# A residual layer with a mean and a condition: another split of the bias, mean and chunk work over four engines

## The chip, the cores and the metric

The kernel runs on one core of one Trainium2 chip, and no other core takes part. The metric is device time in microseconds (us); a comparison uses the median of several executions. One further execution was recorded by the hardware profiler, and all durations of single instructions come from that one.

The engines have two names each here: TensorE is PE in the profile (its weight loads are PEld), VectorE is DVE, ScalarE is ACT, GpSimd is POOL, and SyncE is SP, which only issues transfers. SBUF is the on-chip memory; PSUM is the eight banks that TensorE writes its results to. Each engine executes its own instructions in a fixed order, and waits where an operand is not there yet.

## The reference

`x` is (4, 1024, 512), the condition `c` is (4, 256), `W` is (1536, 512) and `b` is (512), all float32. With `h = concat(c, c)` (4, 512), the reference computes

```
m[r]      = mean over l of x[r, l, :]
out[r, l] = x[r, l] + relu( x[r, l] @ W[0:512] + m[r] @ W[512:1024] + h[r] @ W[1024:1536] + b )
```

So the three last terms are one row of 512 numbers for each of the four rows r of the batch: this row is called the bias of row r below. It can only be finished when all 1024 positions of that row have been read.

## The kernel before, in words

**Tiles.** The 4096 positions are 32 tiles of 128, eight to a row of the batch. A tile's product has four chunks j of the contraction (128 each), and each float32 product is made of three faster ones: x and W are split into a high part (`hi`, `w_hi`) and a rest (`lo`, `w_lo`), and `hi*w_hi + hi*w_lo + lo*w_hi` are added up in a PSUM bank of the tile (`product`, line 459). That makes 12 matmuls of 512 columns for a tile, 3 for a chunk. There are five such banks (`O_BANKS`).

**Chunks.** The left operand has to be transposed. For the first eight tiles TensorE does that (`turn`, line 252) from x as it was loaded; for the others VectorE does it (line 254) in groups of four tiles, from a second load of x in another layout (`z`, 24 transfers of 256 KB, line 191), and writes a PSUM bank (`xT`, two banks). ScalarE takes the high part from there and sums it over the positions as it goes (`split_hi`, 265); VectorE takes the rest (`split_lo`, 281).

**Bias.** For each row, `weigh` (348, ScalarE) and `add_term` (353, GpSimd) make the two condition terms in SBUF (`cond`); `total` (336) and `mean_term` (341), both VectorE, add the four mean terms and leave the result in a PSUM bank (`acc`). `acc_split_hi` (357, ScalarE) and `acc_split_lo` (361, VectorE) split it, and `bias_product` (373, TensorE) spreads it over 128 partitions.

**Bias to tile.** For rows 0 and 1, TensorE adds the bias to the tile's bank with one more matmul (`bias_to_bank`, 470; 13 tiles), and ScalarE's relu empties the bank (480). The first three tiles (`KEEP = 3`) are finished before a bias is there: ScalarE copies them to SBUF (`keep`, 473), and VectorE adds the bias later, both operands in SBUF. For rows 2 and 3 VectorE adds the bias as it empties the bank (`add_bias`, 477) and ScalarE applies the relu. GpSimd adds x (`add_x`, 485), and SyncE stores.

**Order.** The order on each engine is not written by hand. `Plan` (line 19) is a list scheduler that runs when the kernel is built: each step has costs for the engines that may run it, the steps that it depends on, and a number that says how urgent it is; `run` takes the step that can start first by its own clock. The costs and numbers are the kernel's own constants. What comes out is one fixed sequence for each engine, also for SyncE's transfers. A row's bias product is put in TensorE's sequence where the plan's clock has it ready.

**Start.** x tiles 0, 1, 2-3 and 4-7 are loaded from SyncE's queue, the four chunks of W[0:512] from ScalarE's queue (line 202) beside them, the condition `c_sb` and `b_sb` from GpSimd's (146, 149). Eleven matmuls on zeros keep TensorE busy until x is there (144).

Of the kernel before, what the change touches and what calls it, by code (L numbers as in the profile page):

```python
# [12 lines left out]
ALU = mybir.AluOpType  # L13
AX = mybir.AxisListType
PSUM = bass.MemoryType.PSUM
N_WARM = 11


class Plan:
# [3 lines left out]


    HANDOVER = 0.2
    PATIENCE = 0.1
# [5 lines left out]
    def add(self, key, costs, deps, urgency, emit, later=0.0):  # L32


        assert key not in self.todo, key
        self.todo[key] = (costs, list(deps), urgency, emit, later)

    def run(self):
        while self.todo:
            could = []  # L40
            for key, (costs, deps, urgency, _, _) in self.todo.items():
                if not all(d in self.done for d in deps):
                    continue
                options = []
                for engine, cost in costs.items():
                    start = self.free[engine]
                    for d in deps:
                        end, later, by = self.done[d]
                        if by != engine:
                            end += later + self.HANDOVER  # L50
                        start = max(start, end)
                    options.append((start + cost, start, engine, cost))
                _, start, engine, cost = min(options)
                could.append((start, urgency, key, engine, cost))
# [14 lines left out]
def kernel(  # L69
# [8 lines left out]

# [11 lines left out]
    S_BUFS = 15  # L103
    O_BANKS = 5
    Z_BUFS = 3
    X_BUFS = 4
    O_BUFS = 10
    Z_AHEAD, X_AHEAD, T_AHEAD = 24, 8, 7
    TURN_PE = (0, 1, 2, 3)
    BY_PE = 2  # L110
    KEEP = 3
# [4 lines left out]
    spool = ctx.enter_context(tc.tile_pool(name="spool", bufs=S_BUFS))  # L116
    small = ctx.enter_context(tc.tile_pool(name="small", bufs=2))
# [16 lines left out]
    warm = const.tile([P, 512], BF16, name="warm")  # L134
    nc.vector.memset(warm, 0.0)
    ones = const.tile([P, 1], F32, name="ones")
    nc.vector.memset(ones, 1.0)
    table_warm = const.tile([P, 1], F32, name="table_warm")
    nc.scalar.activation(table_warm, ones, AF.Relu)
    ident = const.tile([P, P], F32, name="ident")  # L140
    make_identity(nc, ident)
    pw = ps_b.tile([P, 512], F32, tag="b", name="pw")
    for _ in range(N_WARM):
        nc.tensor.matmul(pw, lhsT=warm[:, :P], rhs=warm, start=True, stop=True)
    c_sb = const.tile([B, H], F32, name="c_sb")
    nc.gpsimd.dma_start(out=c_sb, in_=cond)
    b_sb = const.tile([P, D], F32, name="b_sb")
    nc.gpsimd.memset(b_sb, 0.0)
    nc.gpsimd.dma_start(out=b_sb[0:1, :], in_=b.rearrange("(o d) -> o d", o=1))
    mean32 = const.tile([P, P], F32, name="mean32")  # L150
    nc.gpsimd.memset(mean32, 1.0 / L)
    mean = const.tile([P, P], F32R, name="mean")
    nc.gpsimd.tensor_copy(mean, mean32)


    units = [(0, 0, 1), (0, 1, 1), (0, 2, 2), (0, 4, 4)]
    units += [(r, k, G) for r in range(1, B) for k in range(0, NK, G)]
    unit_of = {(r, k0 + i): u for u, (r, k0, n) in enumerate(units) for i in range(n)}
    last_tile = [r * NK + k0 + n - 1 for r, k0, n in units]
    units_of_row = [[u for u, v in enumerate(units) if v[0] == r] for r in range(B)]  # L160
    by_z = [u for u in range(len(units)) if u not in TURN_PE]

# [4 lines left out]
    first_piece = [min(c for (u, _), c in piece_of.items() if units[u][0] == r) for r in range(B)]  # L167
# [3 lines left out]
    w_x = const.tile([P, J, D], F32, name="w_x")  # L171
    w_mean = const.tile([P, J, D], F32, name="w_mean")

# [22 lines left out]
    SP = 0.72  # L196
    SPZ = 1.3
    for i, n in ((0, 1), (1, 1), (2, 2)):
        load_x(0, i, n)
        plan.done["x", 0, i] = (2.8 + 1.3 * i, 2.0, "sp")  # L200
    for j in range(J):
        nc.scalar.dma_start(out=w_x[:, j, :], in_=Wv[0, :, j])
        plan.done["w", j] = (2.9 + 1.3 * j, 2.0, "sp")
    load_x(1)
    plan.done["x", 1] = (9.8, 2.0, "sp")
    w_cond = xpool.tile([P, 2, KH, D], F32, tag="x", name="w_cond")
    nc.sync.dma_start(
        out=w_cond, in_=W[2 * D : 3 * D].rearrange("(s h p) o -> p s h o", p=P, h=KH)
    )
    plan.done["cond"] = (12.7, 2.0, "sp")  # L210
    nc.sync.dma_start(out=w_mean, in_=Wv[1])
    plan.done["w_mean"] = (15.3, 2.0, "sp")
    plan.free["sp"] = 15.3
    for n, u in enumerate(by_z):
        for i in range(NQ):
            deps = [("turn", c) for c in range(len(pieces)) if n >= Z_BUFS and pieces[c][0] == by_z[n - Z_BUFS]]
            plan.add(("z", u, i), {"sp": SPZ}, deps, units[u][0] * NK + units[u][1] - Z_AHEAD,
                     lambda e, u=u, i=i: load_z(u, i), later=3.0)
    x_order = [0, 1, None] + list(range(2, B * NK // G))
    for n, g in list(enumerate(x_order))[3:]:  # L220
        was = x_order[n - X_BUFS] if n >= X_BUFS else -1
        deps = ([] if was == -1 else [("add_cond", k) for k in range(KH)] if was is None else
                [("finished", was * G + i) for i in range(G)])
        ahead = T_AHEAD + 10 if any(u in TURN_PE for u in (unit_of[divmod(g * G, NK)],)) else X_AHEAD
        plan.add(("x", g), {"sp": 4 * SP}, deps, g * G - ahead,
                 lambda e, g=g: load_x(g), later=3.0)
# [3 lines left out]
    w_lo = const.tile([P, J, D], F32R, name="w_lo")  # L230
    for j in range(J):
        plan.add(("w_hi", j), {"act": 0.62}, [("w", j)], -100 + 2 * j,
                 lambda e, j=j: nc.scalar.activation(w_hi[:, j, :], w_x[:, j, :], AF.Copy))
        plan.add(("w_lo", j), {"dve": 0.69, "pool": 1.33}, [("w_hi", j)], -100 + 2 * j + 1,
# [9 lines left out]
    def turn(c):  # L244
        u, js = pieces[c]
        n = units[u][2]
        v = xT[c] = ps_x.tile([P, G * P], F32, tag="x", name=f"xT{c}")
        if u in TURN_PE:
            for i in range(n):
                x_t = x_tile(last_tile[u] - n + 1 + i).rearrange("p (a j) -> p j a", j=J)  # L250
                for m, j in enumerate(js):
                    nc.tensor.transpose(v[:, (m * n + i) * P : (m * n + i + 1) * P], x_t[:, j], ident)  # L252
        else:
            nc.vector.transpose(  # L254
# [15 lines left out]
    def add_up(c):  # L270
        u, js = pieces[c]
        r, n = units[u][0], units[u][2]
# [5 lines left out]
    def split_lo(c):  # L278
        u, js = pieces[c]
        m = units[u][2] * len(js) * P  # L280
        nc.vector.tensor_tensor(  # L281
            lo[c][:, :m], xT[c][:, :m], hi[c][:, :m].bitcast(F32), ALU.subtract
        )

    for c, (u, js) in enumerate(pieces):
        r, k0, n = units[u]

        urgent = 2 * c - 99.5 if not r else r * NK - T_AHEAD + (c - first_piece[r]) * 0.75
        deps = ([x_here(t) for t in range(last_tile[u] - n + 1, last_tile[u] + 1)]
                if u in TURN_PE else [("z", u, i) for i in range(NQ)])  # L290
        if c:
            deps.append(("turn", c - 1))
        if c >= 2:
            deps.append(("lo", c - 2))
            if len(pieces[c - 2][1]) > 1:
                deps.append(("sum", c - 2))
        if r == 1 and c == first_piece[1]:
            deps.append(("term", 0, KH + J - 1))
        w = n * len(js)
        plan.add(("turn", c), {"pe": 0.12 * w} if u in TURN_PE else {"dve": 0.14 + 0.24 * w}, deps, urgent,  # L300
                 lambda e, c=c: turn(c))
        deps = [("turn", c)]
        if c >= S_BUFS:
            v, js_v = pieces[c - S_BUFS]
            deps.append(("product", last_tile[v], js_v[-1]))
        plan.add(("hi", c), {"act": 0.16 + 0.2 * (len(js) == 1) + 0.108 * w}, deps, urgent,
                 lambda e, c=c: split_hi(c))
        plan.add(("lo", c), {"dve": 0.15 + 0.135 * w}, [("hi", c)], urgent - 0.1,
                 lambda e, c=c: split_lo(c))
        if len(js) > 1:  # L310
            plan.add(("sum", c), {"dve": 0.65}, [("turn", c)], urgent + 0.1, lambda e, c=c: add_up(c))
# [4 lines left out]
    bL = const.tile([P, D], F32, name="bL")  # L316
    acc, acc_hi, acc_lo, totals, terms, biases = {}, {}, {}, {}, {}, {}
    conds = {}

    def turn_cond():  # L320
        nc.vector.tensor_scalar(bL, b_sb, float(L), None, ALU.mult)
# [9 lines left out]
    def add_cond(eng, k):  # L331
        eng.tensor_tensor(wc[:, k], w_cond[:, 0, k], w_cond[:, 1, k], ALU.add)

    def total(r):
        totals[r] = small.tile([P, J], F32, tag="tot", name=f"tot{r}")
        nc.vector.tensor_reduce(totals[r], sums[:, r], AX.X, ALU.add)

    def mean_term(r, j):
        if not j:
            acc[r] = ps_b.tile([P, D], F32, tag="b", name=f"acc{r}")  # L340
        nc.vector.scalar_tensor_tensor(  # L341
            acc[r], w_mean[:, j, :], totals[r][:, j : j + 1], acc[r] if j else conds[r],
            ALU.mult, ALU.add,
        )

    def weigh(r, k):
        terms[r, k] = small.tile([P, D], F32, tag="term", bufs=3, name=f"term{r}_{k}")
        nc.scalar.activation(terms[r, k], wc[:, k], AF.Copy, scale=cT[:, k, r : r + 1])  # L348

    def add_term(r, k):  # L350
        if not k:
            conds[r] = small.tile([P, D], F32, tag="cond", bufs=B, name=f"cond{r}")
        nc.gpsimd.tensor_tensor(conds[r], conds[r] if k else bL, terms[r, k], ALU.add)  # L353

    def acc_split_hi(r):
        acc_hi[r] = small.tile([P, D], F32R, tag="acc_hi", bufs=1, name=f"acc_hi{r}")
        nc.scalar.activation(acc_hi[r], acc[r], AF.Copy)  # L357

    def acc_split_lo(r):
        acc_lo[r] = small.tile([P, D], F32R, tag="acc_lo", bufs=1, name=f"acc_lo{r}")  # L360
        nc.vector.tensor_tensor(acc_lo[r], acc[r], acc_hi[r].bitcast(F32), ALU.subtract)

    pbs, rows = {}, {}
    even32 = const.tile([2 * Q, P], F32, name="even32")
# [219 lines left out]
```

## Time and profile before

| | |
|---|---|
| three executions | 117.69, 117.67, 118.13 us; median 117.69 |
| span of the profiled execution | 115.7 us |
| time around the span (median less span; the page gives no other total for the profiled execution) | 2.0 us |
| mean granted TensorE clock | 0.985 |
| busy: PE, DVE, ACT, POOL | 107.7, 81.0, 53.4, 57.8 us |
| instructions: PE, DVE, ACT, POOL | 466, 114, 122, 55 |
| moved by DMA | 26.31 MB, mean 227 GB/s |

The span runs from the first to the last instruction of the execution. A share of busy time is an average over stages; the chain of waits, which follows the last instruction back to what released it, tells which engine sets the end. In that chain, and in the list of instructions in order of time, each line gives the start, the length, the engine, the tile and the line of code; in the list a bracket behind it gives the idle time before and what ended it.

### The profile page before, as it was taken

To read this page: it belongs to the slowest core of one execution; us is meant where nothing else is said; L and a number is where in the kernel's file an instruction comes from. 1 tells how busy PE (TensorE), PEld (TensorE's weight loads), DVE (VectorE), ACT (ScalarE), POOL (GpSimd) and SP (SyncE) were. 2 spreads that over 40 slices of the span, in tenths; PEclk is the share of its full clock that TensorE was granted. 3 is DMA by queue.
4 is the path that set the end of the run, shared out by engine and by line. 5 is a ranking of instruction groups with operands and counts; after the bars stand their busy time and mean duration, and the time that the engine had idled before them with its cause. 6 is when DMAs were issued, how large, how long until landed. Compare 5 with 4: busy or idle time off the path is not lost.

```text
span 115.7 us, 1477 instructions
## 1 busy us (share of the span) xinstructions
PE 107.7 (93%) x466; PEld 82.9 (72%) x466; DVE 81.0 (70%) x114; ACT 53.4 (46%) x122; POOL 57.8 (50%) x55
## 2 busy tenths in 40 slices
PE   5926999999999999999999999999999999999980
PEld 2415788888766687877766688887888878888870
DVE  1066734399999999976896999939999980632250
ACT  5055547887568460424963542246466140642200
POOL 6507144899809643040893029508354913199400
PEclk9998599999999999999999999999999999999999
DMA  3799999999999959999959999994422422025351
GB/s 109 179 392 396 394 370 198 203 203 205 205 256 281 199 136 207 304 388 390 349 177 213 272 397 407 400 258 176 164 91 106 169 91 91 0 91 222 140 227 45
DMA packets 22999, 26.31 MB, mean 227 GB/s; under 512 B 1228, under 2 KB 13776, under 8 KB 22864
## 3 DMA queue, kind: packets, MB, share of 16 engines
q1 hardware_dynamic: 22352, 25.17, 75.7%
q10 hardware_dynamic: 576, 1.05, 3.1%
q8 instruction: 3, 0.05, 0.2%
q14 instruction: 4, 0.03, 0.1%
q0 software_dynamic: 64, 0.01, 0.0%
HBM read 17.83 MB, written 8.39 MB: 227 GB/s over the span
## 4 chain that ended last, share of the span: by engine, by line
PE 89%; DMA 7%; SPq 1%; DVE 0%; issue 0%
PE po_None L459 77%; DMA x<-in_x_dram 7%; PE po_None L470 4%; PE xT L252 3%; PE po L459 2%; PE pb L373 2%; SPq L178 1%; PE po L455 0%; DVE o L490 0%; PE pt L324 0%
## 5 line engine op out<-in xcount | busy, mean ns | idle before, releaser
L485 POOL TENSOR_TENSOR o<-o,x 128x512 f32<-128x512 f32 x30 | 38.7, 1315 | 38.9 <-ACT o L480 32.1
L459 PE MATMUL po_None<-w_hi,hi 128*128 128x512 f32 x124 | 50.8, 409 | 0.0
L459 PE MATMUL po_None<-w_lo,hi 128*128 128x512 f32 x124 | 49.4, 398 | 0.0
L459 PE MATMUL po_None<-w_hi,lo 128*128 128x512 f32 x124 | 49.3, 398 | 0.0
L459 PEld LDWEIGHTS po_None<-w_hi,hi 128*128 128x128 f32 x124 | 23.5, 190 | 7.1 <-issue 1.6
L459 PEld LDWEIGHTS po_None<-w_hi,lo 128*128 128x128 f32 x124 | 23.6, 190 | 5.7
L459 PEld LDWEIGHTS po_None<-w_lo,hi 128*128 128x128 f32 x124 | 23.6, 190 | 5.0
L281 DVE TENSOR_TENSOR lo<-xT,hi 128x512 fp32r<-128x512 f32 (+1 forms) x34 | 21.9, 647 | 7.2 <-ACT hi L265 7.2
L254 DVE STREAM_TRANSPOSE xT<-z 128x512 f32<-128x512 f32 x24 | 26.2, 1102 | 0.3
L265 ACT ACTIVATE hi<-xT 128x512 fp32r<-128x512 f32 (+1 forms) x34 | 19.3, 571 | 9.3 <-DVE xT L254 5.5
L477 DVE TENSOR_TENSOR o<-po_None,bias 128x512 f32<-128x512 f32 x15 | 9.8, 677 | 12.2 <-ACT bias L379 4.1
L480 ACT ACTIVATE o<-o 128x512 f32<-128x512 f32 x17 | 10.5, 631 | 7.5 <-DVE o L477 7.5
L480 ACT ACTIVATE o<-po_None 128x512 f32<-128x512 f32 x13 | 7.5, 601 | 7.9 <-PE po_None L470 7.9
L341 DVE SCALAR_TENSOR_TENSOR acc<-w_mean,tot,acc 128x512 f32<-128x512 f32 x12 | 9.1, 756 | 0.4
L252 PE MATMUL xT<-ident,x 128*128 128x128 f32 x32 | 6.0, 307 | 3.5 <-DMA x<-in_x_dram 3.5
L252 PEld LDWEIGHTS xT<-ident,x 128*128 128x128 f32 x32 | 5.1, 207 | 4.6 <-issue 2.5
L357 ACT ACTIVATE acc_hi<-acc 128x512 fp32r<-128x512 f32 x4 | 2.4, 600 | 11.9 <-DVE acc L341 11.9
L265 ACT ACTIVATION_READ_ACCUMULATOR hi<-xT 128x1 f32 x32 | 6.4, 201 | 0.0
L353 POOL TENSOR_TENSOR cond<-bL,term 128x512 f32<-128x512 f32 x4 | 5.2, 1303 | 2.0 <-ACT term L348 2.0
L341 DVE SCALAR_TENSOR_TENSOR acc<-w_mean,tot,cond 128x512 f32<-128x512 f32 x4 | 5.7, 1426 | 0.6 <-POOL cond L353 0.3
L348 ACT ACTIVATE term<-wc,cT 128x512 f32<-128x512 f32 x8 | 5.6, 723 | 0.7 <-POOL cond L353 0.7
L353 POOL TENSOR_TENSOR cond<-cond,term 128x512 f32<-128x512 f32 x4 | 5.5, 1383 | 0.3
(54 smaller groups left out, 60.7 us busy)
## 6 DMA issues: line engine op xcount, KB each, us to landing
out_dram<-o SPq DMA_DIRECT2D x31, 256.0 KB, 2.4
x<-in_x_dram SPq DMA_DIRECT2D x7, 1024.0 KB, 7.9
z<-in_x_dram SPq DMA_DIRECT2D x24, 256.0 KB, 7.4
w_x<-in_L_cond_W_dram ACTq DMA_DIRECT2D x4, 256.0 KB, 7.2
w_cond<-in_L_cond_W_dram SPq DMA_DIRECT2D x1, 1024.0 KB, 12.7
w_mean<-in_L_cond_W_dram SPq DMA_DIRECT2D x1, 1024.0 KB, 12.6
x<-in_x_dram SPq DMA_DIRECT2D x2, 256.0 KB, 4.1
x<-in_x_dram SPq DMA_DIRECT2D x1, 512.0 KB, 8.0
```

The lines of the kernel that those rows point to most:

```text
L252: nc.tensor.transpose(v[:, (m * n + i) * P : (m * n + i + 1) * P], x_t[:, j], ident)
L254: nc.vector.transpose(v[:, : n * P].rearrange("p (n t) -> p n t", t=Q), zs[u].rearrange("p n (a j) -> p n j a", j=J)[:, : n * NQ, js[0], :],)
L265: nc.scalar.activation(hi[c][:, :m], xT[c][:, :m], AF.Copy, accum_out=sums[:, r, js[0], s : s + 1] if len(js) == 1 else None,)
L281: nc.vector.tensor_tensor(lo[c][:, :m], xT[c][:, :m], hi[c][:, :m].bitcast(F32), ALU.subtract)
L341: nc.vector.scalar_tensor_tensor(acc[r], w_mean[:, j, :], totals[r][:, j : j + 1], acc[r] if j else conds[r], ALU.mult, ALU.add,)
L348: nc.scalar.activation(terms[r, k], wc[:, k], AF.Copy, scale=cT[:, k, r : r + 1])
L353: nc.gpsimd.tensor_tensor(conds[r], conds[r] if k else bL, terms[r, k], ALU.add)
L459: nc.tensor.matmul(pos[key][:, :w], lhsT=v[p][:, c], rhs=m[:, j, d], start=(h is None and j == 0 and n == 0), stop=((t < KEEP or r >= BY_P ...
L470: nc.tensor.matmul(pos[t], lhsT=even, rhs=rows[t // NK], start=False, stop=True)
L477: nc.vector.tensor_tensor(o, o if t < KEEP else pos[t], biases[t // NK], ALU.add)
L480: nc.scalar.activation(o_tile(t), pos[t] if KEEP <= t < BY_PE * NK else outs[t], AF.Relu)
L485: nc.gpsimd.tensor_tensor(outs[t], outs[t], x_tile(t), ALU.add)
```

## The change

- **Loads.** The chunks of W[0:512] go over SyncE's queue, mixed with the x tiles: x 0, w 0, w 1, x 1, w 2, w 3, x 2-3, x 4-7, then the mean part and the condition part of W. `c_sb` and `b_sb` go over ScalarE's queue. Five warming matmuls stand in place of eleven. ScalarE scales `b_sb` by 1024 in place (`b_row`).
- **Bias to tile.** `bias_to_bank` is gone. Ten tiles are kept in SBUF (`KEEP = 10`); VectorE adds the bias there later. All other tiles but the last get it from VectorE as it empties the bank.
- **Mean terms.** `mean_term` on VectorE is gone: `weigh` (ScalarE) and `add_term` (GpSimd) make six terms for each row in place of two. The sum stays in SBUF, so both splits read it there.
- **Chunks.** The chunks j = 1 and j = 3 of the tiles that VectorE turns go to SBUF (`tpool`, three buffers) and not to PSUM; three of these twelve have their rest taken by GpSimd.
- **Plan.** Due times are in microseconds (`at(t) = 6.0 + 2.82 t`) in place of tile numbers. Pools: five x buffers (one of them first holds w_x), 13 chunk buffers, 14 output buffers. Within a chunk the order is `hi*w_hi`, `lo*w_hi`, `hi*w_lo` by operand names of the code.

```diff
-    S_BUFS = 15
+    S_BUFS = 13
+    T_BUFS = 3
-    X_BUFS = 4
-    O_BUFS = 10
+    X_BUFS = 5
+    O_BUFS = 14
-    BY_PE = 2
-    KEEP = 3
+    KEEP = 10
+    TERMS = 3
+    N_WARM = 5
+    STEP, START = 2.82, 6.0
...
+    in_sbuf = {c for c, (u, js) in enumerate(pieces) if u not in BY_PE and js[0] % 2}
...
-    for j in range(J):
-        nc.scalar.dma_start(out=w_x[:, j, :], in_=Wv[0, :, j])
+    for key in (("x", 0, 0), ("w", 0), ("w", 1), ("x", 0, 1), ("w", 2), ("w", 3), ("x", 0, 2), ("x", 1)):
+        if key[0] == "w":
+            load_w(key[1])
...
+            if c in in_sbuf:
+                v = xT[c] = tpool.tile([P, G * P], F32, tag="t", name=f"xT{c}")
+            else:
+                v = xT[c] = ps_x.tile([P, G * P], F32, tag="x", name=f"xT{c}")
...
-    def mean_term(r, j):
-        if not j:
-            acc[r] = ps_b.tile([P, D], F32, tag="b", name=f"acc{r}")
-        nc.vector.scalar_tensor_tensor(
-            acc[r], w_mean[:, j, :], totals[r][:, j : j + 1], acc[r] if j else conds[r],
-            ALU.mult, ALU.add,
-        )
+    def weigh(r, n):
+        terms[r, n] = small.tile([P, D], F32, tag="term", bufs=TERMS, name=f"term{r}_{n}")
+        if n < KH:
+            v, scale = wc[:, n], cT[:, n, r : r + 1]
+        else:
+            v, scale = w_mean[:, n - KH, :], totals[r][:, n - KH : n - KH + 1]
+        nc.scalar.activation(terms[r, n], v, AF.Copy, scale=scale)
...
+        nc_of[e].tensor_tensor(acc_lo[r], conds[r], acc_hi[r].bitcast(F32), ALU.subtract)
...
+    plan.add(("b_row",), {"act": 0.65}, [], at(1), lambda e: nc.scalar.activation(bL, bL, AF.Copy, scale=float(L)))
...
-    def bias_to_bank(t):
-        nc.tensor.matmul(pos[t], lhsT=even, rhs=rows[t // NK], start=False, stop=True)
...
+            plan.add(("added", t), {"dve": 0.72, "pool": 1.33}, [("freed", t), ("bias", r)], slow, lambda e, t=t: add_bias(e, t))
...
+            plan.add(("freed", t), {"dve": 0.69}, deps + [("bias", r)], free, lambda e, t=t: add_bias(e, t))
```

## The prediction

> **What bounds the kernel now.** I read the page first, then the chain of waits in order of time, then VectorE's and GpSimd's instructions in order of time.
>
> ```profile
> PE   5926999999999999999999999999999999999980
> PEclk9998599999999999999999999999999999999999
> ...
> PE 89%; DMA 7%; SPq 1%; DVE 0%; issue 0%
> ```
>
> TensorE is the bound from 9.8 us on: after the first loads the chain never leaves it. Its clock fell once, in slices 4 and 5. The chain shows what the time consists of:
>
> ```profile
> 9.80 0.48 PE xT L252 x2
> 10.28 2.02 PE po_None L459 x6
> ...
> 36.26 3.00 PE po_None L459 x12
> 39.26 0.43 PE po_None L470
> ...
> 76.44 21.69 PE po_None L459 x93
> ...
> 112.42 0.42 DVE o L490
> ```
>
> 93 matmuls in 21.69 us are 0.2332 us each, so a tile takes 2.80. The last tile, in halves with its bias matmuls, takes 3.33 (109.07 to 112.40). A bias product takes 0.47, a transpose 0.118 (four in 0.47). The sum: first product at 10.28, 372 x 0.2332 = 86.75, last tile 3.33, 22 transposes 2.6, four bias products 1.9, two small transposes of the condition 0.3, and the 13 `bias_to_bank`. From 20.99 to 109.07 there are 88.08 us, of which 345 products take 80.45 and four bias products 1.88; the remaining 5.75 are the price of these 13, their slower neighbours included (12 products in 3.00 in place of 2.80). All that makes 110.9; TensorE ends at 112.40. The missing 1.5 us is the low clock (six products took 2.02 and 1.71 us in place of 1.40). From there 3.3 us to the end of the span (115.7), and 2.0 from the span to the median of 117.69.
>
> The second thing to see is how VectorE and GpSimd meet:
>
> ```profile
> 23.25 1.78 DVE L341 SCALAR_TENSOR_TENSOR acc<-w_mean,tot,cond 128x512 f32<-128x512 f32 x1 [0.31 <-POOL cond L353]
> 43.22 1.82 DVE L341 SCALAR_TENSOR_TENSOR acc<-w_mean,tot,cond 128x512 f32<-128x512 f32 x1
> 68.13 0.76 DVE L341 SCALAR_TENSOR_TENSOR acc<-w_mean,tot,cond 128x512 f32<-128x512 f32 x1
> 90.08 1.36 DVE L341 SCALAR_TENSOR_TENSOR acc<-w_mean,tot,cond 128x512 f32<-128x512 f32 x1
> ```
>
> ```profile
> 43.18 1.29 POOL L485 TENSOR_TENSOR o<-o,x 128x512 f32<-128x512 f32 x1 [1.49 <-ACT o L480]
> ...
> 68.60 5.21 POOL L485 TENSOR_TENSOR o<-o,x 128x512 f32<-128x512 f32 x4 [6.81 <-DMA x<-in_x_dram]
> ...
> 89.58 2.99 POOL L485 TENSOR_TENSOR o<-o,x 128x512 f32<-128x512 f32 x2 [0.94 <-ACT o L480]
> ```
>
> These are the four mean terms whose two big operands both lie in SBUF; the 12 others have one in PSUM and took 0.756 each. At 68.13 GpSimd was idle: 0.76. The other three met a running GpSimd instruction and ended 0.55 to 0.57 after its end (43.18 + 1.29 = 44.47; 43.22 + 1.82 = 45.04). The GpSimd instruction behind was late in turn (two in 2.99 in place of 2.58). So a VectorE instruction with two SBUF operands and a GpSimd instruction take turns: while GpSimd is busy it costs VectorE half of 1.29 + 0.56 = 1.2 us on average, and, directly behind another such one, 1.29 + 0.56 = 1.85, against 0.60 when GpSimd is idle; GpSimd loses about 0.4 each time.
>
> **Part by part, TensorE.** Removing `bias_to_bank` takes off 5.75. The start: before, x 0, w 0 and x 1 had landed by 6.87 (the transposes of x 1 start then), and the four parts x 0, x 1, w 0, w 1 by 8.17 (ScalarE's second `w_hi`). The new order asks for the same four first, x 1 last, and starts products after its transposes without x 2-3, which held up TensorE until 9.67. So x 1 lands between 5.2 (1 MB at the page's 392 GB/s from 2.5 us) and 8.2; I take 6.9 less some time for the w 1 bytes still missing then, plus 0.5 for transposes: first product at 7.2 (5.7 to 8.7). The low clock I leave at 1.5 (0 to 2.5): TensorE again does little before its first product, and fewer warming matmuls run. If nothing ever made TensorE wait, it would end at 7.2 + 86.75 + 3.33 + 24 x 0.118 + 1.9 + 1.5 = 103.5; span 106.8, time 108.8.
>
> **VectorE and GpSimd.** VectorE loses 16 mean terms (9.1 + 5.7 us) and gains 13 bias adds (31 for 18, at 0.68: 8.8), so it has a little less to do. But 22 of its instructions now have two SBUF operands: 10 kept adds, 9 rests of SBUF chunks (the other 3 go to GpSimd), 3 `acc_split_lo`. Before there were 7 once the weights were split: the four above and three kept adds, which met an idle GpSimd (0.67). And GpSimd goes from 42 big instructions to 60 (16 terms, 3 rests and a split more, two `w_lo` less): 60 x 1.30 = 78 us, so it is busy most of the time from the arrival of the condition weights (about 19.4, where the fifth MB landed before) to the end. Kept adds on plain tensor operations with GpSimd running have no row here; I price them like the mean terms, between 0.60 and 1.85, and take 1.5, since they stand in runs.
>
> The Trainium skill (SBUF — State Buffer, section Who interferes with whom) states this rule outright: a VectorE instruction with two SBUF inputs and a GpSimd instruction that reads SBUF exclude each other for the whole instruction, tensor_tensor included. It speaks against this change; by it the sum is the forecast below, without it that of the first rival.
>
> **Where that meets TensorE.** In the order as built, a row's bias product stands in TensorE's sequence at a fixed place: row 0 after 135 products, row 1 after 153, row 2 after 246, row 3 after 339. If `acc_split_lo` is late there, every product behind waits.
> - Row 0: TensorE is there at 7.2 + 31.5 + 2.8 + 1.5 = 43.0. GpSimd has 16 instructions before it (21 us from 19.4 = 40.4, and about 1.5 for waits on terms): 42. No wait (bounds 0 to 2). Bias of row 0 in SBUF at 43.0 + 0.5 + 0.6 = 44.1.
> - Row 1: TensorE is there at 43.5 + 18 x 0.2332 = 47.7. `acc_split_lo` is VectorE's third after the bias, behind two kept adds: 44.1 + 3 x 1.6, and 0.3 as the first finds GpSimd at the start of an instruction: 49.2. Wait 1.5 (0 to 2).
> - Row 2: TensorE is there at 49.2 + 0.47 + 93 x 0.2332 = 71.4. `acc_split_lo` of row 2 is VectorE's 34th after 44.1. Nineteen of these are plain: 9 adds and rests at 0.60, 6 transposes at 1.03, 4 totals at 0.12, 12.1 us. Fifteen have two SBUF operands (ten kept adds, three rests, two splits): 15 x 1.5 = 22.5. Ready at 78.7 (74.4 at 1.2, 84 at 1.85, 65 at 0.60). Wait 7.3. GpSimd is busy all through: its 20 instructions from 44 on and 15 losses of 0.4 are 32 us. This is the term that decides.
> - Row 3: VectorE has 21 us more (13.8 plain, 5 x 1.5), ready at 100; GpSimd is at about 101 with the last term. TensorE comes at 78.7 + 0.47 + 21.7 = 100.9, or 102.6 with the clock below: no wait (0 to 3).
>
> A stop of 7 us is also long enough for the clock to fall: before, TensorE was nearly idle from 5.6 to 9.8, then ran slow in slices 4 and 5 and lost 1.5. I add 1.7 (0 to 3). The Trainium skill (TensorE: Matmul & The Clock Gate, part 1) has one idle window of 3.4 us as the limit; by it a stop under 3.4 us can go without this loss (rival 2 below), and one of 7 cannot, which leaves the sum as it is.
>
> The sum from row 2: 78.7 + 0.47 + 21.7 + 1.7 = 102.6; then 0.47, 9 products 2.1, two tiles 5.6, the last tile 3.33: TensorE ends at 114.1, span 117.4, time 119.4. The rest lies beside it: ScalarE's 16 terms (0.61 apart, 10 us) on an engine busy 46%; SyncE's stores of kept tiles, which come late but find 14 output buffers; x and z loads, which ask for the same bytes in nearly the same order; transposes to SBUF in place of PSUM (1.0 to 1.2 each, 12 of them, 1 us either way).
>
> **Rivals.**
> 1. The turns cost little and TensorE alone is the bound. For: most VectorE instructions today never meet GpSimd, and the three kept adds took 0.67. Against: those met an idle GpSimd. Row 2 is in time if the fifteen cost 1.0 or less each (44.1 + 12.1 + 15 = 71.2). Then 108.8 to 111. The price from which the change is no gain: 119.4 less 1.7 is 117.7, that is 1.7 / 15 = 0.11 less each, 1.4.
> 2. Between: at 1.0 to 1.35 each a part of the gain is left, 111 to 117; at 1.2, 4.3 less wait and probably less clock loss: 114.
> 3. The start goes wrong. ScalarE's sequence has `b_row` in front of the first `w_hi`, and TensorE's has the condition's transposes in front of those of x. These two small loads took 6.3 and 7.0 us before, from another queue. If `b_sb` still needs 6.3 from about 2.1, the first product is at 8.4 + 0.65 + 0.63 = 9.7, 2.5 later, and the bias with it: 122.
>
> **How the numbers follow.** A difference under 0.5% (0.6 us) can hardly be told from none here. Forecast (price near 1.5, 116 to 123.5): 0.52, of which 0.10 lies within 0.5% of the time before. Rival 1: 0.17; rival 2: 0.20, both faster; rival 3: 0.11, slower. So faster 0.37, same 0.10, slower 0.42 + 0.11 = 0.53. The range leaves out half of rival 1 below 110 and about 0.1 above 124, where 1.85 and a late start come together.
>
> **What would show it.** Right: TensorE waits for VectorE's `acc_lo` before the bias product of row 2, some 7 us near 71; kept adds of 1.2 to 1.85 us beside busy GpSimd; first product near 7. Wrong: kept adds of 0.68 while GpSimd runs; no wait of TensorE after 20 us; a first product after 9; or a wait at row 0, which would put the fault on GpSimd's and ScalarE's chain of terms.

## The result: slower by about 4%

The changed kernel takes 122.46 us (median of four, 121.16 to 123.98), beside 117.68 us for the kernel before in the same series: a ratio of 1.044 with an interval of 1.032 to 1.056. The forecast was 119.4 us, slower, with 110 to 124 as the range.

The execution with the profile is the longest of the four (123.98 us, span 122.2; the spans of the other three are 119.3 to 120.8), so its terms sum to more than the median. Two rows of its page and the chain by engine:

```profile
PE   6632999999999999979999999029999999999970
PEclk9999999999999999999999999975599999999999
...
PE 64%; DVE 20%; DMA 7%; issue 3%; ACT 1%; DVEq 0%; ACTq 0%
```

Before, the chain was 89% TensorE and VectorE had no share in it. Now VectorE has 20%, TensorE has a hole in slices 26 and 27, and its clock falls behind the hole. The list of TensorE's instructions in order of time shows the hole (start, length, and in brackets the idle time and its releaser):

```profile
75.92 0.40 PE L437 MATMUL po_None<-w_lo,hi 128*128 128x512 f32 x1
79.43 0.50 PE L378 MATMUL pb<-acc_hi,mean 128*128 128x512 f32 x1 [3.11 <-ACT acc_hi L367]
82.22 0.80 PE L378 MATMUL pb<-acc_lo,mean 128*128 128x512 f32 x1 [2.28 <-DVE acc_lo L371]
82.81 0.63 PE L437 MATMUL po_None<-w_hi,hi 128*128 128x512 f32 x1
83.24 0.63 PE L437 MATMUL po_None<-w_hi,lo 128*128 128x512 f32 x1
```

These two are the bias product of row 2. TensorE was there at 76.15 (75.92 and one spacing) and got the second operand at 82.2: 6.0 us. Then twelve products start 0.427 apart in place of 0.233, another 2.3 us. VectorE's list tells what kept it, and GpSimd's what it met:

```profile
72.49 1.72 DVE L290 TENSOR_TENSOR lo<-xT,hi 128x512 fp32r<-128x512 f32 x2
74.12 5.13 DVE L455 TENSOR_TENSOR o<-o,bias 128x512 f32<-128x512 f32 x3
79.18 2.07 DVE L263 STREAM_TRANSPOSE xT<-z 128x512 f32<-128x512 f32 x2
81.19 0.98 DVE L371 TENSOR_TENSOR acc_lo<-cond,acc_hi 128x512 fp32r<-128x512 f32 x1
```

```profile
73.62 3.42 POOL L363 TENSOR_TENSOR cond<-cond,term 128x512 f32<-128x512 f32 x2
77.00 7.55 POOL L461 TENSOR_TENSOR o<-o,x 128x512 f32<-128x512 f32 x5
```

Three kept adds (the bias added to a tile that is kept in SBUF, both operands there) take 5.13 us and five GpSimd adds 7.55 us, each longer than alone. GpSimd's two terms are the last of row 2's chain: it ends at 77.04, 0.9 us after TensorE had come. By groups (busy time, mean ns of one), kept adds cost twice the adds that read a bank:

```profile
L455 DVE TENSOR_TENSOR o<-po_None,bias 128x512 f32<-128x512 f32 x21 | 13.5, 680 | 7.4 <-PE po_None L437 5.1
L455 DVE TENSOR_TENSOR o<-o,bias 128x512 f32<-128x512 f32 x10 | 14.4, 1465 | 0.9 <-ACT bias L382 0.9
```

The second difference is the start. ScalarE's list, and TensorE's first product:

```profile
3.47 0.25 ACTq L213 DMA_DIRECT2D b_sb<-in_L_cond_b_dram  x1
9.58 0.63 ACT L386 ACTIVATE b_sb<-b_sb 128x512 f32<-128x512 f32 x1 [6.77 <-DMA b_sb<-in_L_cond_b_dram]
10.12 0.61 ACT L233 ACTIVATE w_hi<-w_x 128x512 fp32r<-128x512 f32 x1
```

```profile
11.27 0.80 PE L437 MATMUL po_None<-w_hi,hi 128*128 128x512 f32 x1 [2.56 <-ACT hi L274]
```

w 0 had landed at 5.30, but its split stands behind `b_row`, which waited until 9.58 for the 2 KB of `b_sb`. The chain of waits shows that this load itself was issued only when x 0 had landed:

```profile
0.73 2.66 DMA x<-in_x_dram
3.39 0.02 issue
3.41 0.02 ACTq L213
3.43 0.04 issue
3.47 6.09 DMA b_sb<-in_L_cond_b_dram
```

### The profile page after: what moved, and what is told of

The parts are those of the page before. It is cut to its first block, busy times and chain, and to the rows that moved or that the text cites. A ratio compares the mean times of both kernels' runs of the same rounds, so it can differ in the third digit from the quotient of the medians.

```text
span 122.2 us, 1493 instructions
## 1 busy us (share of the span) xinstructions
PE 105.7 (87%) x447; PEld 83.3 (68%) x447; DVE 86.8 (71%) x118; ACT 68.1 (56%) x145; POOL 86.7 (71%) x69
## 4 chain that ended last, share of the span: by engine, by line
PE 64%; DVE 20%; DMA 7%; issue 3%; ACT 1%; DVEq 0%; ACTq 0%
PE po_None L437 57%; DVE o L455 8%; DMA b_sb<-in_L_cond_b_dram 5%; DVE xT L263 5%; DVE lo L290 4%; PE xT L257 2%; PE po L437 2%; DVE acc_lo L371 2%; DMA x<-in_x_dram 2%; PE pb L378 2%; ACT b_sb L386 1%; ACT bias L382 0%; ACT w_hi L233 0%; DVE w_lo L240 0%; PE po L433 0%
## 5 line engine op out<-in xcount | busy, mean ns | idle before, releaser
L461 POOL TENSOR_TENSOR o<-o,x 128x512 f32<-128x512 f32 x30 | 43.3, 1471 | 5.1 <-ACT o L458 5.1
L290 DVE TENSOR_TENSOR lo<-xT,hi 128x512 fp32r<-128x512 f32 (+1 forms) x31 | 25.4, 829 | 9.9 <-ACT hi L274 9.8
L363 POOL TENSOR_TENSOR cond<-cond,term 128x512 f32<-128x512 f32 x20 | 28.3, 1421 | 1.7 <-ACT term L358 1.0
L458 ACT ACTIVATE o<-o 128x512 f32<-128x512 f32 x30 | 18.6, 630 | 13.0 <-DVE o L455 13.0
L455 DVE TENSOR_TENSOR o<-po_None,bias 128x512 f32<-128x512 f32 x21 | 13.5, 680 | 7.4 <-PE po_None L437 5.1
L345 POOL TENSOR_TENSOR wc<-w_cond 128x512 f32<-128x512 f32 x2 | 2.5, 1288 | 18.5 <-DMA w_cond<-in_L_cond_W_dram 18.5
L455 DVE TENSOR_TENSOR o<-o,bias 128x512 f32<-128x512 f32 x10 | 14.4, 1465 | 0.9 <-ACT bias L382 0.9
L358 ACT ACTIVATE term<-w_mean,tot 128x512 f32<-128x512 f32 x16 | 11.2, 718 | 3.3 <-DVE tot L350 3.3
L363 POOL TENSOR_TENSOR cond<-b_sb,term 128x512 f32<-128x512 f32 x4 | 5.6, 1410 | 4.4 <-ACT term L358 4.4
L240 DVE TENSOR_TENSOR w_lo<-w_x,w_hi 128x512 fp32r<-128x512 f32 x4 | 2.6, 687 | 5.0 <-ACT w_hi L233 5.0
```

The costliest lines, as they stand in the source:

```text
L240: lambda e, j=j: nc_of[e].tensor_tensor(w_lo[:, j, :], w_x[:, j, :], w_hi[:, j, :].bitcast(F32), ALU.subtract))
L290: nc_of[e].tensor_tensor(lo[c][:, :m], xT[c][:, :m], hi[c][:, :m].bitcast(F32), ALU.subtract)
L358: nc.scalar.activation(terms[r, n], v, AF.Copy, scale=scale)
L363: nc.gpsimd.tensor_tensor(conds[r], conds[r] if n else bL, terms[r, n], ALU.add)
L455: nc_of[e].tensor_tensor(o, o if t < KEEP else pos[t], biases[t // NK], ALU.add)
L458: nc.scalar.activation(outs[t], outs[t], AF.Relu)
```

## Experiments

Theory: VectorE's instructions with two SBUF operands take turns with GpSimd, so row 2's `acc_split_lo` comes late; the start is a second, separate cost. Rivals: GpSimd's own chain of terms is what is late; or the start explains it all. Ratios are to the kernel before, run beside each on the same chip; the changed kernel stands at 1.044.

**1. `b_row` behind the splits of W.** The changed kernel with one dependency:

```diff
-    plan.add(("b_row",), {"act": 0.65}, [], at(1), ...
+    plan.add(("b_row",), {"act": 0.65}, [("w_hi", J - 1)], at(1), ...
```

> The changed kernel, with ScalarE's scaling of the bias row (b_row) put behind its four w_hi instead of in front of them; the order is otherwise nearly the same. The theory of turns (a VectorE instruction with two SBUF operands and a GpSimd instruction exclude each other, and that makes row 2's bias late): the first product moves from 11.3 to about 8.7, but the stop at row 2 stays at 5 us or more, since the terms on GpSimd and the adds on VectorE start little earlier: 120 to 121.5 us, still slower than before. The rival that the late start is the loss: 2.6 us less and more, below 119, and little stop left.

Measured: 1.0171 (1.0082 to 1.0261). The first product moves from 11.27 to 8.32, and row 2's stop stays (idle 2.66 and 2.29 us), with the low clock behind it:

```profile
76.50 0.50 PE L378 MATMUL pb<-acc_hi,mean 128*128 128x512 f32 x1 [2.66 <-ACT acc_hi L367]
79.29 0.80 PE L378 MATMUL pb<-acc_lo,mean 128*128 128x512 f32 x1 [2.29 <-DVE acc_lo L371]
```

So the start is worth about 2.7% (the intervals leave 1.2 to 4.2) and does not explain the rest. The time, 119.7 us at the first series' 117.68, lies between the theory's 120 and the rival's 119; it is the stop that speaks for the theory.

**2. `b_sb` loaded earlier.** The changed kernel, the tile cleared by VectorE first of all:

```diff
+    nc.vector.memset(b_sb, 0.0)
+    nc.scalar.dma_start(out=b_sb[0:1, :], ...)
     warm = const.tile([P, 512], BF16, name="warm")
...
-    nc.gpsimd.memset(b_sb, 0.0)
-    nc.scalar.dma_start(out=b_sb[0:1, :], ...)
```

> The changed kernel, with the load of b_sb issued near 1.4 us in place of 3.5 (VectorE clears the tile first of all, and the issue stands in front of ScalarE's table load); nothing else moves. In the changed kernel it landed at 9.56, 6.1 us after its issue and behind x 0, w 0 to w 3 and x 1, which were issued before it on SyncE's queue and had landed by 9.37. Theory (a small load waits for the large ones issued before it, whatever its queue): with x 0, w 0 and perhaps w 1 ahead of it, it lands between 3.5 and 6.9, the first w_hi starts by 7.5 and the first product near 8.3, as where b_row stood behind the splits (8.32, 1.0171): ratio 1.01 to 1.025. Rival (this load of 2 KB takes its 6 us whatever is ahead): it lands at 7.5 to 8, first product 9 to 9.5, ratio 1.02 to 1.035. In both the stop before row 2's bias product stays, 4 to 6 us.

Measured: 1.0254 (1.0156 to 1.0351). Issued at 1.43, it has landed by 3.72:

```profile
1.43 0.23 ACTq L205 DMA_DIRECT2D b_sb<-in_L_cond_b_dram  x1
...
3.72 0.63 ACT L386 ACTIVATE b_sb<-b_sb 128x512 f32<-128x512 f32 x1 [0.53 <-DMA b_sb<-in_L_cond_b_dram]
```

It takes at most 2.3 us in place of 6.1, so the 6 us are not this load's own. (The ratio alone does not part the two sides; the landing does.) The first product starts at 8.00, 3.3 us sooner, but the time falls by 1.9% (2.2 us) only. TensorE now waits 3.29 us at row 1 (0.89 in the changed kernel), and its clock falls there as well:

```profile
48.55 0.49 PE L378 MATMUL pb<-acc_hi,mean 128*128 128x512 f32 x1
52.33 0.80 PE L378 MATMUL pb<-acc_lo,mean 128*128 128x512 f32 x1 [3.29 <-DVE acc_lo L371]
```

At row 2 it stops for 4.2 us. Part of an earlier start is spent waiting for VectorE; in number 1 the wait at row 1 was 2.10. (The two gains themselves lie within each other's intervals.)

**3. GpSimd's adds of x cut to 64 columns.**

```diff
-        nc_of[e].tensor_tensor(outs[t], outs[t], x_tile(t), ALU.add)
+        nc_of[e].tensor_tensor(outs[t][:, :64], outs[t][:, :64], x_tile(t)[:, :64], ALU.add)
```

> The changed kernel, but GpSimd adds only 64 of 512 columns of x (the rest of x is left out of the output); VectorE's instructions and their order are unchanged. Turns: with GpSimd mostly idle, the kept adds and the rests of SBUF chunks fall from about 1.4 to 0.6 to 0.9 us, TensorE no longer stops at row 2 (now 6.1 us) and its clock stays full after it (now 2.3 lost): about 114 us. The rival that these VectorE instructions are slow by themselves, with both operands in SBUF: they stay near 1.4, the stop stays, 121 to 122.5.

Measured: 0.9695 (0.9611 to 0.978). The median kept add takes 0.81, and TensorE goes through row 2's bias product without a stop (its two matmuls start at 76.52 and 76.92). The late first product is still in it (about 11.3), so what GpSimd's adds of x do to the others is worth more than the whole loss. This alone does not part the turns from GpSimd's being less busy.

**4. GpSimd as busy, but writing.** In place of each add of x, two memsets of the tile and the add of 64 columns:

```diff
-        nc_of[e].tensor_tensor(outs[t], outs[t], x_tile(t), ALU.add)
+        nc_of[e].memset(outs[t], 0.0)
+        nc_of[e].memset(outs[t], 0.0)
+        nc_of[e].tensor_tensor(outs[t][:, :64], outs[t][:, :64], x_tile(t)[:, :64], ALU.add)
```

> The changed kernel, with each of GpSimd's adds of x replaced by two memsets of the whole output tile (0.53 us each) and an add of 64 of the 512 columns; the output is wrong in the sense that x and the relu are left out of 448 columns. GpSimd is busy as long as before but reads almost nothing. Theory (only a GpSimd instruction that reads SBUF excludes a VectorE instruction with two SBUF operands): kept adds of 0.65 to 0.9 beside the memsets, no stop before row 2's bias product, ratio 0.965 to 0.985, as with the short adds (0.9695). Rival (any GpSimd instruction excludes, or the write port is what is shared): kept adds 1.1 to 1.5, a stop of 3 to 6 us, ratio 1.01 to 1.045.

Measured: 1.0253 (1.0101 to 1.0405), where the theory had 0.965 to 0.985. Its mechanism is seen, its time is not. GpSimd is busy for 83.7 us (86.7 in the changed kernel), and the kept adds are short. By the summary of the output tiles (min, median, max in ns):

```profile
L455 DVE TENSOR_TENSOR o<-o,bias x10: 674/680/1782, 48.7 to 70.8; 128x512 f32<-128x512 f32 x10
```

Beside memsets they take 0.67 to 0.69; the slow ones lie beside terms of 512 columns, which read. At row 2 TensorE passes at 75.40 without a wait, and the chain of terms, with its adds less delayed, is in time as well (it ends at 74.12, in the changed kernel at 77.04). But at row 3, which it now reaches 8.7 us sooner, it waits for GpSimd's chain of terms, whose last ends at 100.2 behind more memsets, and the clock falls once more:

```profile
100.94 0.79 PE L378 MATMUL pb<-acc_hi,mean 128*128 128x512 f32 x1 [2.58 <-ACT acc_hi L367]
```

So reading is what makes VectorE wait, and a GpSimd that is busy for 84 us holds TensorE up by itself, one row further on. The ratio lies in the rival's range, but not for the rival's reason: beside instructions that only write, no kept add waits.

**5. All chunks to PSUM.**

```diff
-    in_sbuf = {c for c, (u, js) in enumerate(pieces) if u not in BY_PE and js[0] % 2}
+    in_sbuf = set()
```

> The changed kernel, with all twelve chunks that went to SBUF going to PSUM again; their rests (split_lo) then have one operand in PSUM and do not take turns with GpSimd. The plan redoes the order: row 0's bias product stands after 120 products, row 1's after 147, row 2's after 252. Theory (turns): between row 0's bias (45.6) and row 2's acc_split_lo VectorE has 11 instructions with two SBUF operands in place of 15, at 1.46, and 27 plain ones (6 adds and 9 rests at 0.6 to 0.7, 8 transposes at 1.03, 4 totals at 0.12), 34.5 us, ready at 80; TensorE comes at 77, so it waits 3 there in place of 6.1, and the clock may hold: ratio 1.00 to 1.03 beside 1.044 for the changed kernel. The late first product (11.3) stays. Rival (the chunks in SBUF are no part of it; GpSimd's chain of terms is late): the stop stays 6, ratio 1.035 to 1.055.

Measured: 1.0384 (1.0274 to 1.0493), above the theory's range and within the rival's. VectorE's stage runs from 46.87 to 80.08, 33.2 us as expected (34.5), but TensorE, there at 76.7, then waits for a bank too: it is idle 1.41 and 1.38 us before the two operands and 1.69 before the bank, less than the rival's stop of 6. GpSimd's last term of row 2 ends at 77.07, later than TensorE came here too. Five kept adds stand back to back, at 1.62 each:

```profile
46.87 8.09 DVE L455 TENSOR_TENSOR o<-o,bias 128x512 f32<-128x512 f32 x5
```

The chunks in SBUF are not shown to matter: the difference from 1.044 lies within the intervals. This run does not decide between theory and rival.

**6. Mean terms back on VectorE.**

```diff
-        else:
-            v, scale = w_mean[:, n - KH, :], totals[r][:, n - KH : n - KH + 1]
...
+        nc.vector.scalar_tensor_tensor(
+            acc[r], w_mean[:, j, :], totals[r][:, j : j + 1], acc[r] if j else conds[r],
+            ALU.mult, ALU.add,
+        )
```

> The changed kernel, with the four mean terms of each row back on VectorE and summed in a PSUM bank as before; GpSimd keeps 8 condition terms and loses 16 mean terms (some 23 us of its time), and the kept adds stay on VectorE. Theory (turns, VectorE's queue sets row 2): VectorE has 6 us more of mean terms between the biases of row 0 and row 2, the kept adds still meet GpSimd's adds of x (1.2 to 1.5 each, since GpSimd is now idle part of the time), so the stop before row 2's bias product stays between 3 and 8 us: ratio 1.02 to 1.06. Rival (GpSimd's chain of six terms a row is what is late): with the chain gone TensorE's stop is under 1.5 us, ratio 0.99 to 1.01.

Measured: 1.056 (1.0406 to 1.0713). The rival's 0.99 to 1.01 falls: GpSimd is relieved (69.4 us busy) and the kernel is no faster. But the stop is not where the theory put it: at row 2's bias product TensorE does not wait at all, as the rival had it. It waits for two `lo` rests that the plan gave to GpSimd, behind its adds of x, and for banks:

```profile
PE po_None L451 <- POOL lo L290: 3.6, 2, 1.9
PE po_None L451 <- DVE o L469: 2.9, 2, 1.5
```

The plan redid its order, so this run does not undo one part cleanly, and it does not show what the chain of terms costs.

**7 and 8. The kernel before with one part each.** First without any `bias_to_bank` (`BY_PE = 0`, row 0's and row 1's bias added by VectorE):

> The kernel before with one part of the change alone: no bias_to_bank, VectorE adds the bias as it empties the bank in all rows (BY_PE = 0; three tiles kept as before, mean terms and chunks as before). These adds have one operand in PSUM. Turns: 5.75 us come off TensorE and the adds, about 0.6 each, lie beside GpSimd's work: 111 to 113.5 us. The rival that more adds on VectorE are too much wherever their operands lie: 116 to 119, with TensorE waiting at a bias product or for a bank.

Measured: 0.9862 (0.9761 to 0.9962), which is 116.1 us at the first series' 117.68: less gain than expected, and the rival's side, with waits for a bank. VectorE has no gap from 34 to 66 us, and TensorE waits for its adds:

```profile
PE po_None L459 <- DVE o L477: 3.9, 5, 1.8
```

Against the 5.75 us that went stand 3.9 of waits for banks.

Second, the kernel before with the new order of loads over SyncE's queue; `b_sb` stays on GpSimd's queue:

> The kernel before with the other part alone: x and w_x over SyncE's queue in the mixed order of the change, and the plan told when they land in the changed kernel, so that the first products stand ahead of the transposes of tiles 2-3. b_sb stays on GpSimd's queue and VectorE scales it. First product at 6.5 to 7.5 in place of 10.28, part of it lost to the low clock: 114 to 116.5 us. The rival that one queue feeds no faster: 117 to 118.5.

Measured: 0.9853 (0.976 to 0.9947). That is 116.0 us on the same scale, as expected. The first product starts at 6.96, near the 7.2 that the prediction had; no `b_row` stands in front of it.

**9. A version faster than both.** The loads of 8, and `BY_PE = 1`: the bias of row 1 by VectorE, that of row 0 (5 tiles) still by TensorE.

```diff
-    BY_PE = 2
+    BY_PE = 1
```

> The kernel before, with two parts of the change: its first loads in the new order over SyncE's queue (b_sb stays on GpSimd's queue), and VectorE adds the bias of row 1 as it empties the banks, so 8 of the 13 bias_to_bank go; row 0 keeps its 5, which spares VectorE 3.4 us in the stage from 36 to 50 us that was too full for it without them. Kept tiles, mean terms and chunks are as before. Theory: the loads give 1.5 to 1.8 us, 8 x 0.44 = 3.5 us of bias_to_bank go, and TensorE waits 0 to 1.5 us for banks: ratio 0.957 to 0.972, faster than both kernels and than either part alone (0.985, 0.986). Rival (VectorE is full from 36 to 66 us whatever row 0 does): waits of 3 us for banks, ratio 0.975 to 0.985.

Measured: 114.53 us, 0.9768 (0.9676 to 0.9861): in the rival's range, but with waits of 0.7 us for the rival's 3, and not told apart from either part alone. A second time beside number 10:

> The version that leaves row 0's bias to TensorE and gives row 1's to VectorE, with the new order of loads, run a second time beside the version without any bias_to_bank. Theory: 0.970 to 0.982, as in its first run (0.9768), with TensorE waiting under 1 us in all behind 20 us of the span. If the first run was by chance: nearer to 0.985, as each part alone.

Measured: 114.03 us, 0.9671 (0.9584 to 0.9758). This time the interval lies below the measured ratio of either part alone. In the second profile TensorE is not made to wait behind 12 us of the span (0.7 us in all in the first); its chain by engine:

```profile
PE 91%; DVE 3%; issue 1%; ACT 1%; DVEq 0%
```

**10. The same without row 0's `bias_to_bank` as well** (`BY_PE = 0`).

> The kernel before, with the first loads in the new order over SyncE's queue and no bias_to_bank at all: VectorE adds the bias of row 0 (5 tiles) too as it empties the banks. Against the version that left row 0 to TensorE (0.9768). Theory (VectorE has no room from 36 to 50 us): the 5 bias_to_bank saved there, 2.2 us, are given back as waits for banks of 2 to 4 us, ratio 0.970 to 0.985, no better than 0.9768. Rival (the loads part had set the limit; the gains add): waits under 1 us, ratio 0.955 to 0.968.

Measured: 0.9955 (0.9906 to 1.0005), worse than either side expected. TensorE again waits 3.9 us in five waits for VectorE's adds. Five small matmuls of 0.44 us taken off TensorE cost 3.4 us (117.42 beside 114.03), and they cost it in the stage where VectorE is full: in the two profiles the 121st product starts at 44.06 and 44.03 us, the 161st at 57.52 and 53.81. That the earlier start brings nothing here beside number 7 fits VectorE as the bound of that stage, but their intervals do not tell the two apart.

## Why the prediction was right, and where it was off

The direction was right, and so was the mechanism: TensorE stopped before row 2's bias product, where VectorE's instructions with two SBUF operands had taken turns with GpSimd. That the time came out near is in part luck: a start that was too early in the sum went against waits that were too long in it. And one of the signs that the prediction had named as wrong came true, a first product after 9: its rival 3 (a chance of 0.11, 122 us) happened on top of the forecast. By its own steps, against the profiled execution:

- **First product: 7.2 predicted, 11.27 measured.** This is the step that was off most. I took the landing of x 1 (6.9 predicted, 7.54 measured) as what the first product waits for. What it waits for was written down as rival 3: `b_row` in front of the first `w_hi`. I gave that a chance of 0.11, and its size was low as well: I put the issue of `b_sb` at 2.1, and it came at 3.47. ScalarE's table load (1.28 us) in front of it had ended at 2.59; what it waited for after that was x 0, which landed at 3.39. Experiments 1 and 2 show the cause, each by moving that load or its user alone; with it out of the way the first product came at 8.32 and 8.00, still 0.8 or more behind 7.2.
- **Low clock at the start: 1.5 predicted, 2.6 measured** (first product to row 0's bias product took 36.9 us, where 135 products and 24 transposes are 34.3). The row PEclk shows no fall there; that the clock was low is read from the products, which start 0.427 apart until 15.3, as behind the hole. With the first term, TensorE reaches row 0 at 48.2 in place of 43.0.
- **Row 0: no wait, as predicted.** With the first product at 8.0 (experiment 2) TensorE came at 43.64 and did not wait either.
- **Row 1: wait 1.5 predicted, about 1.1 measured** (0.89 idle). With the first product at 8.0 it was 3.3 (experiment 2), so for the start that I had assumed my 1.5 was too small.
- **Row 2: 7.3 predicted, 6.0 measured.** VectorE took 32.7 us from the first kept add to the end of `acc_split_lo`, where the sum had 34.6. Kept adds averaged 1.465; counted from start to start, the fifteen instructions with two SBUF operands took 21.0 us, 1.40 each where I had 1.5. Rival 1 is out. But 1.40 is the very price that I had named as the point of no gain, and rival 2 ended at 1.35, so the price alone does not decide the direction. Experiments 1 and 2 do: with the first product near 8 they are still slower than the kernel before, by 1.7 and 2.5%. (At a price of 1.2 my bound should read 74.2 in place of 74.4.) One thing was missing from the step: 3.1 us of the idle time ended with ScalarE's `acc_hi`. It stood in its queue behind relus that waited for the kept adds, but it also needed GpSimd's last term, which ended at 77.04. With 0.6 for `acc_hi` and 0.7 for `acc_split_lo` behind that (my estimate from the rows), TensorE would have waited some 2.2 of the 6.0 us for GpSimd's chain even with VectorE free. The turns are in that chain too: its last two terms took 1.7 us each in place of 1.3.
- **Low clock behind the stop: 1.7 predicted, 2.3 measured** over twelve products, and 0.4 more in the bias product.
- **Row 3: no wait, as predicted.** Experiment 4 suggests that this rested on the stop at row 2: without it, and with GpSimd as busy as that, TensorE waits 2.6 us there.
- **The end:** 0.4 us more than the 3.3 that I carried over. The last add ended 0.45 us behind TensorE, as before, so the 0.4 us lie behind it, with the last stores. The last full `relu_add_x`, which has two SBUF operands as well, took 1.74 us beside GpSimd (0.69 before) and sent its store off late; what part that has is not shown.

Against the forecast: 5.2 later at row 0, 0.4 less wait at row 1, 1.3 less at row 2, 1.0 more low clock, which is 4.5; TensorE ends at 118.5 where the forecast had 114.1. The median lies 3.1 us above the forecast. Experiments 1 and 2 moved the first product by 3.0 and 3.3 us and gained 3.2 and 2.2 us, so the start accounts for most of that, or all of it, as far as the intervals (1.8 us either way) allow.

The Trainium skill (SBUF — State Buffer, section Who interferes with whom) limits its rule to a GpSimd instruction that reads SBUF; one that only writes is left out. Experiment 4 agrees: 0.67 to 0.69 us beside memsets, where the changed kernel's kept adds averaged 1.465 beside instructions that read.

The Trainium skill (TensorE: Matmul & The Clock Gate, part 1) gives one idle window of 3.4 us as what lowers the clock, and I had read it as leave for any shorter stop. The rows do not allow that reading: in experiment 5 no idle time there was over 1.7 us, three of them lay between 76.7 and 82.3, and the products behind them started 0.43 apart until 85.05; in experiment 2 a wait of 3.29 us was followed by twelve slow products, and in experiment 4 one of 2.58 us by eleven. Neither several short stops in a row nor a single one somewhat below 3.4 us were free here.

What stays open: the mean terms and the chunks were only undone inside a plan that reorders everything, so their own share is not known. How the stop at row 2 divides between VectorE's queue and GpSimd's chain is an estimate; no run held one of them fixed. Nor was it tried whether the changed kernel would gain if kept adds were placed behind `acc_split_lo`.

## What to carry to other kernels

Before moving work to an engine because it has idle time, count what its operands will meet: an add with both operands in SBUF cost 0.67 us beside an idle GpSimd and 1.47 on average beside one that reads, and it was the sum over ten of them and five other such instructions, around one urgent chain, that stopped TensorE. Look at the stage and not at the kernel: the same exchange of a small matmul for a VectorE add lost 3.4 us in row 0 and gained in row 1 (from 0.985 to 0.977 and 0.967, the first of these within the intervals). And in every engine's sequence, look at what stands first: one scaling, which waited for a load of 2 KB, held all splits of W.

## What was not expected of the hardware

A load of 2 KB took 6.1 us from another queue when it was issued at 3.47, after 1.5 MB of larger loads of which only x 0 had landed, and at most 2.3 us when issued at 1.43, after 0.5 MB. Experiment 2 expected as much, but I had not allowed for it in the sum. Its reason, that a small load waits for the large ones issued before it, is not the whole of it: w 0 was issued before that early load, at 1.18, and its split, which starts as soon as it has landed, came only at 5.18, when the 2 KB had been there for 1.5 us.

GpSimd pays for the turns as well: its adds of x averaged 1.47 us (1.32 before). Of the 30, twelve took 1.71 to 1.84 us and the others about 1.3; before, one took 1.74.
